# Where the second half of the queries and keys is set down on its way through a two-layer transformer kernel

## The chip, the cores and the metric

The kernel is one program on one core of a Trainium2 chip, written in Tile. A core has five engines that share an on-chip memory (SBUF, 128 partitions) and work through their own queues, each in its own order: TensorE (PE: matrix products, with weight loads listed apart as PEld), VectorE (DVE), ScalarE (ACT), GpSimd (POOL) and SyncE (SP), which here only issues transfers (DMA). TensorE's products go to a second memory (PSUM), from which VectorE and ScalarE take them here. The metric is the device time of one execution in microseconds (us).

## The reference, cut to what matters

A model width of 256, four sequences of 512 tokens, two layers, each an attention and a feed-forward part behind a layer norm, with residual sums:

```python
x = x + attn0(layernorm(x))   # 16 heads of 16, causal softmax over 512 tokens
x = x + ffn0(layernorm(x))    # 8 experts, weights from the two largest of a softmax per output column
x = x + attn1(layernorm(x))   # 16 heads of 128, 4 groups of keys and values
x = x + ffn1(layernorm(x))    # gated, 2048 wide, weights unpacked from 4 bits
```

The change lies in `attn0`, of which this is what counts:

```python
qkv = einsum('bsd,od->bso', x, w_project).reshape(b, s, 3, 16, 16)
q, k, v = transpose(qkv, (2, 0, 3, 1, 4))
att = softmax(where(causal, -1e9, einsum('bhqd,bhkd->bhqk', q, k) / 4), axis=-1)
out = einsum('bhqk,bhkd->bhqd', att, v)          # then a projection by w_out
```

## The kernel before, in words

The tokens are cut into four blocks (`NBLK`, j = 0 to 3) of 128 tokens from each of the four sequences. The attention of layer 0 runs in 44 batches, numbered n: block 0 has one batch for each sequence, block 1 two, blocks 2 and 3 four, since a later block has more keys and a batch then takes fewer groups of heads. A batch goes through `greatest` (scores, L647), `mask` (L660, with the row maxima on VectorE, L666), `shift` (a transposition `mxT`, L676, and the subtraction from the queries, L679), `powers` (the scores anew, L695, exponentials on ScalarE, L704, the mask on GpSimd, L714) and `mixed` (products with the values, `av`, L731). At the end of a sequence `divided` normalises (`av_T`, L749; `oq_T`, L766; a copy into `aT`, L769), and after the last sequence projects (`o`, L778, added to `xres` on VectorE, L788).

The rest of layer 0's work is filled in between. Python generators ("streams") yield pieces with a planned cost; `fill` takes pieces from them at fixed points of the loop over batches. The order of every engine's instructions is thus written out while the program is built (`manual_schedule`), and each engine keeps to it. A late instruction holds all that stands behind it on its engine. Streams that matter here:

- `prepare(j)` for blocks 2 and 3: layer norm, transposition (L582), then `projections(j)`.
- `fold_pieces`: adds the biases into the router's and the experts' weights (TensorE L252, VectorE L258). It reads the tile `rows`.
- `weight_pieces`: the experts' weights from the router's logits. Its first step writes `hi4` (VectorE, L371).
- `result_pieces`: the experts' products (`eo`, L234), scaled by ScalarE into `part` (L323), which VectorE adds up (L350 to L352).

`projections(j)` makes the block's queries and keys in two halves of the heads, `half` 0 and 1. Each half has two calls of `project`, i = 0 (keys) and 1 (queries). A call makes a product of 128 by 512 (`qk_ps`, two steps, L545), and ScalarE copies it from PSUM into the tile `stage` (L549). After the second call eight transfers (L555) carry the half from `stage` into its places in `qk`, where four heads lie at partitions 0, 32, 64 and 96. They are issued by SyncE (for block 0 half of them by ScalarE) and are 64 KB each.

`stage` has the size of 4 KB a partition and comes from the pool `a1`, which has one buffer for a tag. A tile of the same tag can be written only when all readers of the one before are done: here, when its eight transfers have landed. Block 0's first half alone is elsewhere (`unused`, in the space of the logits).

The pool `b1` holds the space of the experts, also one buffer for each tag. Two of its tags have 4 KB a partition as well: `hi4`, first used for the biases (`bs`), and then by `weight_pieces` from token group 0 on; and `part`, first used for `rows`, and then by `result_pieces`.

The products `qk_ps`, `oq_T`, `av_T`, the folds, the logits (`lg_ps`), the experts' products and `o` share two buffers of PSUM (`ps_dn`), so that a product can start when the last but one has been emptied. The scores have five buffers, of which four are filled at a time, and `mxT` and `av` share one.

Of the kernel before, what the change touches and what calls it, by code (L numbers as in the profile page):

```python
# [8 lines left out]
F32 = mybir.dt.float32  # L9
# [7 lines left out]
P = 128  # L17
# [15 lines left out]
def tile_transformer(  # L33
# [71 lines left out]
    b1 = w_ffn0.enter_context(tc.tile_pool(name="f0_1", bufs=1, side="right"))  # L105
# [8 lines left out]
    def need(engine, cost, gap=0, cond=None):  # L114
        return engine, cost, gap, cond
# [333 lines left out]
    with ExitStack() as l0:  # L449
# [90 lines left out]
        def project(j, xT, half, stage, i):  # L540

            at = 256 * (1 - i) + 128 * half
            ps = ps_dn.tile([P, 512], F32, tag="dn", name=f"qk_ps{j}_{half}_{i}")
            for hc in range(2):
                nc.tensor.matmul(  # L545
                    ps, lhsT=wp[:, hc, at : at + P],
                    rhs=xT[:, hc].rearrange("p s q -> p (s q)"), start=hc == 0, stop=hc == 1,
                )
            nc.scalar.copy(stage[:, i], ps)  # L549
            if i:  # L550
                to = 4 + j % 2
                for r in range(8):
                    h = 32 * (r % 4)
                    eng = nc.scalar if j == 0 and r % 2 else nc.sync
                    eng.dma_start(  # L555
                        out=qk[h + 4 : h + 20, 2 * half + r // 4, j : to + 1 : to - j].rearrange(
                            "p i s q -> p i (s q)"
                        ),
                        in_=stage[16 * r : 16 * r + 16],
                    )  # L560

        def values(j, xT, s):

            ps = ps_dn.tile([P, 2, HID], F32, tag="dn", name=f"v_ps{j}_{s}")
            for i in range(2):
                for hc in range(2):
                    nc.tensor.matmul(
                        ps[:, i], lhsT=xT[:, hc, s + i], rhs=wp[:, hc, 512:768],
                        start=hc == 0, stop=hc == 1,
                    )  # L570
            at = j * per_block
            to = va[:, at : at + per_block].rearrange("p (s h d) -> p s h d", s=NS, d=17)
            nc.scalar.copy(
                to[:, s : s + 2, :, 0:16], ps.rearrange("p s (h d) -> p s h d", d=16)
            )
# [14 lines left out]
        def projections(j, xT):  # L590
            if j > 1:
                for s in (0, 2):
                    yield need("PE", 1.75, 1, cond=lambda: blanked > 5 * j - 10)
                    values(j, xT, s)
            for half in range(2):
                if j or half:
                    stage = a1.tile([P, 2, 512], F32, tag="stage", name=f"stage{j}_{half}")
                else:
                    stage = unused("stage0", "p (i q) -> p i q", i=2)
                for i in range(2):  # L600

                    yield need(
                        "PE", 1.75, 0 if half or i else 1,
                        cond=lambda: j < 2 or done >= 8 * j - 12 and blanked >= 5 * j - 5,
                    )
                    project(j, xT, half, stage, i)
                if half == (not j) and j < 2:
                    for s in (0, 2):
                        yield need("PE", 1.75)
                        values(j, xT, s)  # L610

        def prepare(j):

            out = []
            yield from norm_pieces(
                j, b1, b2, out, cond=lambda: j == 2 or inputs[2].next is None
            )
            xT = a1.tile([P, 2, NS, P], F32, tag="xT0", name=f"xT0_{j}")
            yield from inputs_T(j, out[0], xT)
            yield from projections(j, xT)  # L620

        def unused(name, pattern, **sizes):

            tile = b2.tile([P, NE, HID], F32, tag="lg", name=name)
            return tile.rearrange("p e o -> p (e o)")[:, :1024].rearrange(pattern, **sizes)
# [188 lines left out]
        for piece in projections(0, xT):  # L814
            pass
# [3 lines left out]
        greatest(0)  # L819
        mask(0)  # L820
        inputs = {1: Stream(projections(1, xT))}
        done = blanked = 0
        fold = Stream(fold_pieces())
# [4 lines left out]
        for n in range(NBT):  # L828
            j, s, gs = batches[n]
# [92 lines left out]
    with ExitStack() as l1:  # L922
# [198 lines left out]
        for p in range(-1, NP):  # L1121
            j, kv = divmod(p, NKV)
# [179 lines left out]
```

## Time and profile before

| | us |
|---|---|
| median of 3 runs | 1177.23 |
| lowest, highest | 1175.32, 1181.05 |
| the profiled execution: its own time | 1182.05 |
| its span, first to last instruction | 1180.3 |
| TensorE busy in it | 1148.1 |
| VectorE busy | 809.7 |
| ScalarE busy | 484.3 |
| GpSimd busy | 108.1 |

The profiled execution's mean TensorE clock was 0.993 of full speed. The copies into `stage` (16 of them) start between 15.1 and 155.5 us of the span, and the transfers out of it between 17.4 and 161.0 us; a copy takes 586 ns, a transfer 2.4 us from its issue to its landing (median). So the change concerns the first seventh of the span; layer 0's attention and all that follows come after it.

How to read the rows of the profile that follow: a row of the timeline has the start in us, the duration in us (of all merged instructions), the engine, the line of the kernel, the operation, the tiles (output, then inputs), shapes and the number of instructions, and in brackets how long the engine sat idle before it and what ended this. A row of the waits has the engine and line that waited, what it waited for, and the total in us, the number of times and the longest. A row of the table by stretches has the stretch, its length, and for PE, PEld, DVE, ACT and POOL the busy time with the number of instructions; then the granted TensorE clock, the share of the DMA engines and the rate in GB/s.

### The profile page before, as it was taken

The page shows a single profiled execution, that of the slowest core. Times are in us where ns is not written, and L with a number is a line of the kernel's source. Part 1 is how long each engine was busy: PE and PEld are TensorE (multiplying, and loading weights), DVE is VectorE, ACT ScalarE, POOL GpSimd, SP SyncE. Part 2 cuts the span into 40 slices and gives each one's busy share as a digit, 9 for nine tenths or more (in the row PEclk, how much of TensorE's full clock was granted, in tenths as well). Part 3 has the DMA queues.
Part 4 walks back from the last instruction along what each step waited for, and adds up shares of the span by engine and source line. Part 5 has one row for each costly group of instructions (what it writes and reads, how often), then busy time and mean ns, then how long its engine had stood idle before and what let it go on. Part 6 is the DMA issues. An engine that isn't in the chain of part 4 may idle for free.

```text
span 1180.3 us, 18580 instructions
## 1 busy us (share of the span) xinstructions
PE 1148.1 (97%) x7178; PEld 663.9 (56%) x7178; DVE 809.7 (69%) x1783; ACT 484.3 (41%) x1099; POOL 108.1 (9%) x152
## 2 busy tenths in 40 slices
PE   7999989999999899999999999999999999999998
PEld 3656545555555445555555556565644465485487
DVE  5656869999989872867872685687599844725710
ACT  1434545555565453444444443555244312303300
POOL 7313212111111100000000000000000000000000
PEclk9989989999999999999999999999999999999999
DMA  7320010000000320000000001020020000000000
GB/s 217 68 67 12 10 28 1 1 1 2 2 1 2 113 66 1 1 1 1 1 1 1 1 1 45 19 58 24 21 50 3 0 1 18 0 1 18 1 13 23
DMA packets 21239, 26.46 MB, mean 22 GB/s; under 512 B 5128, under 2 KB 14600, under 8 KB 21152
## 3 DMA queue, kind: packets, MB, share of 16 engines
q1 hardware_dynamic: 20480, 24.10, 7.6%
q10 hardware_dynamic: 672, 1.18, 0.4%
q8 instruction: 56, 0.92, 0.3%
q14 instruction: 31, 0.25, 0.1%
HBM read 18.97 MB, written 2.10 MB: 18 GB/s over the span
## 4 chain that ended last, share of the span: by engine, by line
PE 79%; DVE 15%; ACT 2%; issue 2%; POOL 1%; DMA 1%; SPq 0%; ACTq 0%; DVEq 0%; POOLq 0%
PE qk_ps L982 11%; PE y L1229 9%; PE o L1073 9%; PE g L911 9%; PE u L911 9%; PE lg_ps L234 8%; PE eo L234 7%; DVE mx L666 3%; PE s L647 3%; PE s L695 3%; PE av L731 2%; PE qk_ps L545 2%; PE v_ps L964 2%; PE a L1053 1%; PE s L995 1%
## 5 line engine op out<-in xcount | busy, mean ns | idle before, releaser
L982 PE MATMUL qk_ps<-xT,wqkv 128*128 128x512 f32 x320 | 148.9, 599 | 2.3 <-ACT part L323 1.2
L234 PE MATMUL lg_ps<-rw,xT 128*128 128x512 f32 x256 | 122.5, 601 | 1.3 <-ACT xT L949 0.3
L234 PE MATMUL eo<-ew,xT 128*128 128x512 f32 x256 | 121.5, 600 | 0.8 <-ACT lg L297 0.5
L1073 PE MATMUL o<-wpj,oT 128*128 128x256 f32 x512 | 119.1, 382 | 0.0
L1229 PE MATMUL y<-wd,it 128*128 128x256 f32 x512 | 111.8, 379 | 0.0
L1073 PEld LDWEIGHTS o<-wpj,oT 128*128 128x128 f32 x512 | 95.9, 190 | 27.5 <-issue 14.3
L1229 PEld LDWEIGHTS y<-wd,it 128*128 128x128 f32 x512 | 97.0, 190 | 15.0 <-issue 2.2
L666 DVE TENSOR_REDUCE mx<-s 128x1 f32<-128x384 f32 (+3 forms) x176 | 100.4, 631 | 1.4 <-PE s L660 1.4
L982 PEld LDWEIGHTS qk_ps<-xT,wqkv 128*128 128x128 f32 x320 | 59.1, 190 | 71.4 <-issue 57.4
L704 ACT ACTIVATE pt<-s 128x512 f32<-128x512 f32 (+1 forms) x176 | 84.1, 564 | 36.3 <-PE s L695 36.3
L911 PE MATMUL g<-xT,wgu 128*128 128x512 f32 x192 | 90.4, 593 | 0.0
L911 PE MATMUL u<-xT,wgu 128*128 128x512 f32 x192 | 90.2, 592 | 0.0
L323 ACT ACTIVATE part<-eo,c 128x256 f32<-128x256 f32 x128 | 53.6, 472 | 84.7 <-PE eo L234 77.1
L714 POOL TENSOR_SCALAR_AFFINE_SELECT pt<-pt 128x256 f32<-128x256 f32 (+2 forms) x88 | 62.8, 720 | 261.9 <-ACT pt L704 261.3
L1207 ACT ACTIVATE th<-sq 128x512 f32<-128x512 f32 x64 | 40.3, 630 | 87.6 <-DVE sq L1206 87.6
L234 PEld LDWEIGHTS lg_ps<-rw,xT 128*128 128x128 f32 x256 | 46.1, 190 | 46.1 <-issue 37.3
L234 PEld LDWEIGHTS eo<-ew,xT 128*128 128x128 f32 x256 | 46.1, 190 | 45.7 <-issue 38.3
L222 DVE TENSOR_TENSOR xres<-xres,y 128x256 f32<-128x256 f32 x16 | 6.7, 421 | 92.5 <-PE y L1229 92.5
L185 POOL TENSOR_TENSOR ln_rs<-rs_v,minus_half 128x4 f32<-128x4 f32 x16 | 17.6, 1100 | 552.2 <-DVE rs_v L184 439.8
L297 ACT COPY lg<-lg_ps 128x512 f32<-128x512 f32 x64 | 37.6, 588 | 73.5 <-PE lg_ps L234 73.5
L1208 DVE SCALAR_TENSOR_TENSOR th<-th,g 128x512 f32<-128x512 f32 x63 | 43.1, 684 | 29.3 <-ACT th L1207 29.2
L911 PEld LDWEIGHTS u<-xT,wgu 128*128 128x128 f32 x192 | 36.5, 190 | 45.9 <-issue 44.7
(233 smaller groups left out, 1784.4 us busy)
## 6 DMA issues: line engine op xcount, KB each, us to landing
qk<-stage SPq DMA_DIRECT2D x56, 64.0 KB, 2.4
wqkv<-in_w_qkv SPq DMA_DIRECT2D x8, 320.0 KB, 6.6
rw<-in_router_w SPq DMA_DIRECT2D x8, 256.0 KB, 6.9
ew<-in_expert_w SPq DMA_DIRECT2D x8, 256.0 KB, 5.0
wpj<-in_w_proj SPq DMA_DIRECT2D x1, 2048.0 KB
out<-xres SPq DMA_DIRECT2D x4, 512.0 KB, 2.6
xres<-in_x SPq DMA_DIRECT2D x3, 512.0 KB, 8.5
dq_wgu<-in_gate_w SPq DMA_DIRECT2D x8, 128.0 KB, 2.4
```

Source lines behind the costliest of these rows:

```text
L234: nc.tensor.matmul(ps, lhsT=xT[:, hc, (g % 4) * P : (g % 4 + 1) * P], rhs=w[:, hc, 2 * pair : 2 * pair + 2, :].rearrange("p e o -> p (e o) ...
L297: nc.scalar.copy(lg[:, 2 * pair : 2 * pair + 2, :].rearrange("p e o -> p (e o)"), ps)
L323: nc.scalar.mul(part[:, e % 4], ps[:, i], c[:, e : e + 1])
L666: nc.vector.tensor_reduce(maxes[n % 2][:, h, gs[0] : gs[0] + nb], ps[:, : nb * nk].rearrange("p (b k) -> p b k", b=nb), AX.X, ALU.max,)
L704: nc.scalar.activation(pt[:, i, : nb * nk], tiles[2 * pair + i][:, : nb * nk], AF.Exp, scale=0.25)
L714: nc.gpsimd.affine_select(out=last, in_=last, compare_op=ALU.is_ge, fill=0.0, base=0, pattern=pattern, channel_multiplier=-1,)
L911: nc.tensor.matmul(ps, lhsT=wgu[:, w, half, jj, par * P : (par + 1) * P], rhs=xT[:, half, :], start=half == 0, stop=half == 1,)
L982: nc.tensor.matmul(ps, lhsT=wqkv[:, hc, kv, h, :], rhs=xT[:, hc, :], start=hc == 0, stop=hc == 1,)
L1073: nc.tensor.matmul(ys[t // 2][:, t % 2], lhsT=state["o"][:, h, t * P : (t + 1) * P], rhs=wpj[:, HPK * kv + h, :], start=kv == 0 and h == 0 ...
L1207: nc.scalar.activation(th, sq, AF.Tanh, scale=0.7978845608028654)
L1208: nc.vector.scalar_tensor_tensor(th, th, 1.0, gp, ALU.add, ALU.mult)
L1229: nc.tensor.matmul(ps, lhsT=it[:, c // 2, c % 2, t * P : (t + 1) * P], rhs=wd[:, c // 2, c % 2, :], start=c == 0, stop=c == 2 * NJ - 1,)
```

## The change

The second halves of blocks 2 and 3 no longer take the one `stage` buffer of `a1`. The second half of block 2 is set down in the buffer of the tag `hi4`, and that of block 3 in the buffer of the tag `part`, both in `b1`. First halves and the second half of block 1 stay in `stage`. The size and the layout within the tile, the copies and the transfers are as before.

```diff
             for half in range(2):
-                if j or half:
+                if j > 1 and half:
+
+                    stage = b1.tile(
+                        [P, 2, 512], F32, tag="hi4" if j == 2 else "part", name=f"stage{j}_1"
+                    )
+                elif j or half:
                     stage = a1.tile([P, 2, 512], F32, tag="stage", name=f"stage{j}_{half}")
                 else:
                     stage = unused("stage0", "p (i q) -> p i q", i=2)
```

With it the users of a buffer stand in another row. `hi4`: the biases, then the half of block 2, then the first `hi4` of `weight_pieces`. `part`: `rows`, then the half of block 3, then the first `part` of `result_pieces`. `stage`: the second half of block 1, then the first half of block 2, then the first half of block 3. The order of instructions on the engines and on SyncE is the same as before; what differs is what some of them wait for.

## The prediction

> **What bounds the kernel now.** I read the page first, for the engine that is busy and for its clock; then the waits of the stretch in which the change lies; then the instructions in order of time around the two longest of those waits; last a table of short stretches, for the clock.
>
> The page (busy share by engine; mean granted TensorE clock in 40 slices of 29.5 us):
>
> ```profile
> PE 1148.1 (97%) x7178; PEld 663.9 (56%) x7178; DVE 809.7 (69%) x1783; ACT 484.3 (41%) x1099; POOL 108.1 (9%) x152
> ...
> PEclk9989989999999999999999999999999999999999
> ```
>
> TensorE is the bound nearly everywhere, so time is to be had only where it stands still or runs slowly. Its clock is below nine tenths in two slices only, the third (59 to 89 us) and the sixth (148 to 177 us). The waits between 55 and 175 us (engine and line waited for: total us, times, longest):
>
> ```profile
> DVE qk L679 <- PE mxT L676: 18.4, 4, 10.9
> ...
> ACT stage L549 <- DMA qk<-stage: 9.3, 2, 4.7
> ...
> DVE ew L258 <- PE fold L252: 6.1, 2, 4.9
> PE qk_ps L545 <- ACT stage L549: 6.0, 2, 3.2
> ```
>
> Two waits of the copy into `stage` for transfers out of `stage` make two waits of TensorE for that copy, and VectorE waits behind TensorE. The first in order of time (start us, duration), with the undisturbed first half of block 2 ahead of it for comparison:
>
> ```profile
> 68.42 0.38 PE L766 MATMUL oq_T<-ident,oq 128*128 128x128 f32 x2
> 68.64 1.88 PE L545 MATMUL qk_ps<-xT,wp 128*128 128x512 f32 x4
> ...
> 71.68 1.17 PE L695 MATMUL s<-qk 32*128 32x128 f32 x32
> ...
> 76.98 0.38 PE L766 MATMUL oq_T<-ident,oq 128*128 128x128 f32 x2
> ...
> 79.57 0.59 ACT L549 COPY stage<-qk_ps 128x512 f32<-128x512 f32 x1 [4.58 <-DMA qk<-stage]
> ...
> 80.21 3.78 PE L545 MATMUL qk_ps<-xT,wp 128*128 128x512 f32 x4 [2.85 <-ACT stage L549]
> ...
> 86.21 1.18 PE L695 MATMUL s<-qk 32*128 32x128 f32 x32
> ```
>
> The same four matmuls take 1.88 us at 68.64 and 3.78 us at 80.21. The wait costs twice: TensorE stands, and then runs at half speed. The second place is block 3:
>
> ```profile
> 148.14 0.39 PE L766 MATMUL oq_T<-ident,oq 128*128 128x128 f32 x2
> ...
> 151.09 0.59 ACT L549 COPY stage<-qk_ps 128x512 f32<-128x512 f32 x1 [4.71 <-DMA qk<-stage]
> ...
> 151.73 3.78 PE L545 MATMUL qk_ps<-xT,wp 128*128 128x512 f32 x4 [3.20 <-ACT stage L549]
> ...
> 158.25 1.99 PE L778 MATMUL o<-wo,aT 128*128 128x256 f32 x8
> ```
>
> The clock by stretches (the figure after POOL's) gives how long half speed lasts:
>
> ```profile
> 78.00:80.00 2.00, 0.00 (x0) 0.00 (x0) 1.56 (x3) 0.43 (x1) 0.00 (x0) 0.86 0.21 37
> 80.00:82.00 2.00, 1.79 (x2) 0.84 (x3) 0.00 (x0) 0.43 (x2) 0.00 (x0) 0.50 0.00 0
> ...
> 86.00:88.00 2.00, 2.00 (x43) 1.62 (x36) 0.00 (x0) 0.90 (x3) 0.00 (x0) 0.93 0.53 89
> ...
> 150.00:152.00 2.00, 0.27 (x1) 0.27 (x2) 2.00 (x9) 0.91 (x4) 0.00 (x0) 0.78 0.08 13
> ...
> 156.00:158.00 2.00, 2.00 (x40) 1.58 (x36) 0.00 (x0) 0.40 (x2) 0.00 (x0) 0.51 0.20 30
> ```
>
> A mean of 0.86 over 2 us at the levels 1.0 and 0.5 is 0.56 us of half speed, so it begins at 79.44; 0.93 gives its end, 86.28. Likewise 151.12 to 157.96. Each lasts 6.84 us.
>
> **The change: what it removes.** In blocks 2 and 3 the second half's copy no longer waits for the first half's eight transfers. Nothing is added or moved: each engine and SyncE keep their instructions and their order, so no queue is passed and no transfer added. The copies (586 ns) only write elsewhere.
>
> First place. Undisturbed, `oq_T` to the score matmuls of L695 takes 71.68 - 68.42 = 3.26 us; here it takes 86.21 - 76.98 = 9.23. Gain 5.97 us: 3.01 is standing (80.21 - 76.98, less the usual 68.64 - 68.42 = 0.22), 2.96 is half speed (86.21 - 80.21 = 6.00, against 71.68 - 68.64 = 3.04). What is late next, if the copy isn't? Its matmuls ran from 73.28 to 75.16 and ScalarE's exponentials end at 74.99, so it runs at 75.2 and ends at 75.8; `oq_T` at 76.98 and the fold of VectorE that ends at 76.69 are no later than before. Then projection at 77.2, `av` at 79.2, L695 at 80.2; the maxima that free its score banks end at 79.56, 0.7 us earlier. VectorE stood 4.89 us for a fold and 3.62 us for L778, so it follows.
>
> Second place. From the projection the neighbour at 140.83 takes 1.87 us to `av`; `av` of 24 matmuls takes 0.79 (165.01 to 165.80), L695 0.88 (143.71 to 144.59): 3.54 us. With 0.22 from `oq_T` that is 3.76 against 158.25 - 148.14 = 10.11. Gain 6.35 us: 3.37 standing, 2.98 half speed. Late next: the projection's matmuls end at 146.96, so the copy runs from 147.0 to 147.6; six sums of L415 follow it on ScalarE (2.41 us, their last input made at 148.5) to 150.0, then the copy of `aT` to 150.4, which L778 needs at 151.9: 1.5 us to spare. Maxima end at 150.55, L695 starts at 151.0. VectorE has done its work at 152.3 and stood 10.86 us for `mxT` at 162.75; that comes at 156.4, and it still stands some 4 us.
>
> Together 6.4 us standing and 5.9 us half speed: 12.3. At both places the other engines wait behind TensorE too and no load from memory is due, so nothing later keeps its old time and the gain reaches the end. The saving is covered by no other work.
>
> **The waits it adds.** (a) The first `hi4` of the experts' weights (L371, VectorE, 128.54; all of VectorE queues behind it) waits for the transfers out of the stage of block 2. These are issued from about 80 to 86.5 and land 2.4 us later: over 30 us to spare. (b) The first product of the experts (L323, ScalarE, 171.82, so 165.5 on the same scale with the second gain) waits for the transfers of block 3's: copy done at 151.0, eight issues in 6.2 us as from 156.20 to 162.37, landing 2.4 later, 159.6: 5.9 us to spare. (c) In block 2 `oq_T` takes the PSUM bank of the copy at 75.2 to 75.8 (1.1 us early), and the projection after it that of the fold ending at 76.69 (0.5 us early). Missing these costs the excess alone, 0 to some 0.5 us. I take 0 for all.
>
> **Row against rule.** The half-speed term is where a rule speaks against me. The Trainium skill, "TensorE: Matmul & The Clock Gate", "Why this matters for your kernels", asks for no TensorE gap over about 3 us; its "What's actually happening" puts the drop after an idle window of about 3.4 us. The first gap is 77.36 to 80.21, 2.85 us: by the rule no clock is lost and the sum is 6.4. The rows show the clock lost at both places, so I use 12.3. The same section says the windows run free at 3413 ns. This trace agrees: half speed lasts 6.84 us, two windows, and its two starts lie 71.68 us apart, 21.0 windows. The window that ends at 79.44 held 2.08 us of standing and was enough. So whether a gap costs clock depends on how it falls into windows, and can differ from run to run.
>
> **The number.** Against the profiled execution's own time, 1182.05 us (span 1180.3 and 1.75 around it): 1169.7. It stands 4.8 above the median of the runs, 1177.23, and those span 1175.32 to 1181.05, 5.7 us, about what two losses of 3.0 would make. I read the standing (6.4) as in every run and the clock loss as by chance. If 2.08 us in one window is needed, a gap of 2.85 us meets that in 0.62 of the phases, one of 3.2 us in 0.72 (estimates from the gaps and the window); 1.3 losses of 3.0 are 4.0 in the median run. 1177.2 - 6.4 - 4.0 = 1166.8, which I call 1167.
>
> **Rivals.** (1) The median run carries no clock loss: gain 6.4, 1170.8. For: the rule, and that the median lies far below the profiled run. Against: both gaps lose clock in the one run that shows it. (2) One stall comes back in another form, at the tightest point: `aT` behind the six sums on ScalarE holds L778, or a PSUM bank holds the projection. One place yields little: gain 3 to 6, about 1172.5. Against: the margins above; a lateness costs its excess only. (3) Slower: the borrowed `part` tile. L323 waits for eight transfers, ScalarE's queue behind it stops, TensorE runs out of PSUM banks and loses its clock again (3 us). It begins to cost when the transfers land over 5.9 us later than 159.6, and eats the whole gain when they hold L323 by 9.3 us, that is 15 us late: 17.7 us to land, where the slowest of `stage` took 4.0. Held for 15.2 us it makes about 1183. (4) That the change doesn't act: excluded as far as the copy waits only for its matmul and for tiles long done (zeros of the biases, folds before 90 us).
>
> **How the numbers follow.** The forecast 0.77, by itself 1162.5 to 1169.5; rival 1 0.12; rival 2 0.08; rival 3 0.03. Range: below, both clock losses in the median run (1164.9) less 3 for the spread between runs; above, rival 1 and half of rival 2: 1162 to 1172.5. Half a per cent, about what a measurement of this kernel can tell from no change, is 5.9 us, 1171.3. Faster: 0.77, two thirds of rival 1 and a quarter of rival 2, 0.87; same 0.10; slower 0.03.
>
> **What would show it.** Right: no wait of `stage` for DMA after 55 us; a clock of 1.00 in every stretch from 60 to 170; the projection 0.2 us after `oq_T` at both places and 1.9 us long; L371 and L323 waiting for no DMA; a profiled span near 1168. Wrong: a clock below 1.00 there though TensorE has no gap; `aT` or a PSUM bank as the new releaser of TensorE; L323 released by `stage`; a gain at 90 us or 160 us that is no longer there at 400.

## The result, and the profile after

The changed kernel takes 1170.42 us (median of 4 runs, 1169.60 to 1170.83), the kernel before 1177.14 (4 runs, 1175.32 to 1181.05): a ratio of 0.994, 95% interval 0.9919 to 0.9962. Set against 31 runs of the kernel before on one chip, whose median is 1178.77, it is 0.9925 (0.9908 to 0.9941) at 1170.31. So it is faster by 7 to 9 us, 0.6 to 0.75 per cent. The forecast said 1167; the range of all its cases was 1162 to 1172.5.

In the page of the changed kernel, TensorE is busy 6.1 us less, and no slice of its clock is below nine tenths (mean granted clock 1.000, before 0.993; span 1168.6 us, before 1180.3):

```profile
PE 1142.0 (98%) x7178; PEld 661.5 (57%) x7178; DVE 809.8 (69%) x1783; ACT 484.3 (41%) x1099; POOL 108.4 (9%) x152
...
PEclk9999999999999999999999999999999999999999
```

The waits from 55 to 165 us (total us, times, longest). The lines are five later than before, so L684 is the former L679, and L700, L771 and L783 are L695, L766 and L778:

```profile
DVE qk L684 <- PE mxT L681: 12.0, 4, 4.9
...
ACT stage L549 <- PE qk_ps L545: 5.3, 6, 1.6
...
ACT part L323 <- PE eo L234: 3.8, 2, 3.4
...
DVE ew L258 <- PE fold L252: 1.2, 1, 1.2
```

In this stretch `stage` now waits for its products alone, never for a transfer. TensorE's wait for the copy is gone, VectorE's longest wait for `mxT` fell from 10.9 to 4.9, and that for the fold from 4.9 to 1.2. L323, the next user of `part`, waits for its product and not for the borrowed space, and L371, the next user of `hi4`, does not wait for a transfer when it first writes there, at 123.2 us. The two places in the timeline (start, duration):

```profile
77.59 0.38 PE L771 MATMUL oq_T<-ident,oq 128*128 128x128 f32 x2
...
77.81 1.88 PE L545 MATMUL qk_ps<-xT,wp 128*128 128x512 f32 x4
...
80.85 1.17 PE L700 MATMUL s<-qk 32*128 32x128 f32 x32
```

```profile
142.77 0.39 PE L771 MATMUL oq_T<-ident,oq 128*128 128x128 f32 x2
...
143.00 1.88 PE L545 MATMUL qk_ps<-xT,wp 128*128 128x512 f32 x4
...
146.49 1.99 PE L783 MATMUL o<-wo,aT 128*128 128x256 f32 x8
```

From `oq_T` to L700 3.26 us, where it took 9.23; from `oq_T` to L783 3.72, where it took 10.11. Together 12.36 us. The span is only 11.7 shorter, because this execution reached the first place 0.61 us later than the one before (77.59 against 76.98), ahead of anything the change touches. From L783 on both take the same: 1168.6 - 146.49 = 1022.1 and 1180.3 - 158.25 = 1022.1. Nothing is given back in the remaining seven eighths.

So the two profiled executions agree with the sum. What doesn't agree is the time without a profile: 7 to 9 us, not 12. The experiments ask where the difference lies.

### The profile page after: what moved, and what is told of

The parts are those of the page before. It is cut to its first block, busy times and chain, and to the rows that moved or that the text cites. A ratio compares the mean times of both kernels' runs of the same rounds, so it can differ in the third digit from the quotient of the medians.

```text
span 1168.6 us, 18563 instructions
## 1 busy us (share of the span) xinstructions
PE 1142.0 (98%) x7178; PEld 661.5 (57%) x7178; DVE 809.8 (69%) x1783; ACT 484.3 (41%) x1099; POOL 108.4 (9%) x152
## 4 chain that ended last, share of the span: by engine, by line
PE 81%; DVE 13%; ACT 2%; issue 1%; POOL 1%; DMA 0%; SPq 0%; ACTq 0%; DVEq 0%; POOLq 0%
PE qk_ps L987 11%; PE y L1234 9%; PE o L1078 9%; PE g L916 9%; PE u L916 9%; PE lg_ps L234 8%; PE eo L234 7%; PE s L652 3%; PE s L700 3%; DVE mx L671 3%; PE av L736 2%; PE v_ps L969 2%; PE qk_ps L545 2%; PE a L1058 1%; PE s L1000 1%
## 5 line engine op out<-in xcount | busy, mean ns | idle before, releaser
L323 ACT ACTIVATE part<-eo,c 128x256 f32<-128x256 f32 x128 | 53.7, 472 | 85.2 <-PE eo L234 75.2
```

The costliest lines, as they stand in the source:

```text
L323: nc.scalar.mul(part[:, e % 4], ps[:, i], c[:, e : e + 1])
```

## The experiments

"Standing" is the time in which TensorE does nothing because the copy is late; a "loss" is what half speed costs after it. Theory A: the standing is in every run of the kernel before; the half speed is in some runs, more or less of it, by how the gaps fall into the clock's windows. Theory B: both are in every run. Theory C: part of the gain is given back further on.

**The changed kernel again, for the clock of every run** (no edit).

> The changed kernel once more, for the clock of every run of it and of the kernel before. Theory A (standing is saved in every run, the clock loss only where a run of before had it): every run of the changed kernel at clock 1.000 and within 1.5 us of 1170.4; runs of before spread over some 6 us, and their times follow their clocks: about 1176.5 at 1.000, about 1179 with one loss (0.997 to 0.998), about 1182 with two (0.993 to 0.995); median difference 6 to 9 us. Theory B (both losses occur in every run of before, and the profiled execution was long for another reason): before at 0.993 to 0.995 in every run, times without relation to the clock. Theory C (the standing is given back further on): a run of before at clock 1.000 lies within 3 us of the changed kernel.

Measured: all 6 runs of the changed kernel at a granted clock of 1.000, 1169.18 to 1170.64. The kernel before, by the clock of each run; these are the 31 runs of this experiment and 50 made beside later ones:

| mean clock of the run | runs | median us | lowest, highest |
|---|---|---|---|
| 1.000 | 6 | 1175.68 | 1175.24, 1176.34 |
| 0.999 | 7 | 1178.33 | 1176.99, 1178.76 |
| 0.996 to 0.998 | 56 | 1178.25 | 1176.33, 1181.06 |
| 0.994 to 0.995 | 7 | 1180.31 | 1179.74, 1180.93 |
| 0.993 | 5 | 1181.85 | 1181.72, 1182.16 |

The time follows the clock (correlation -0.82). The mean clock is a coarse measure: 3.41 us at half speed take 0.0015 from it (3.41 x 0.5 / 1177), and half speed after TensorE's last product counts as well, so that 0.999 can be one loss (the first of the two further executions below) or none (the run with 11 products). Only 5 of 81 runs are like the profiled one, and 6 show no loss. That is A, and B is out. A run without loss still stands 5.4 us above the changed kernel (1175.68 - 1170.31), more than the 3 that C allowed, so C is out. Over all 81 the mean is 1178.59: 2.9 us of clock loss in the average run.

**Each half of the change alone.**

```diff
-                if j > 1 and half:
+                if j == 2 and half:      # the other run: j == 3
```

> Only block 2's second half set down in hi4; block 3's stays in stage. Theory A: 3.0 us of standing saved in every run and the chance of one clock loss gone: 3 to 4.5 us under the median of before, runs at clock 1.000 or 0.997 to 0.998 and never 0.993. Theory C: less than 1.5 us. In the profile: no wait of stage for DMA near 79 us, the one near 146 as before, about 4.7 us on ScalarE and 3.2 us on TensorE.

> Only block 3's second half set down in part. Theory A: 3.4 us of standing saved in every run, 3.4 to 5 us under the median of before; with the run of block 2 alone it adds up to the whole change, 6 to 9 us. If block 3's borrowed tile costs something (L323 held), this one gains less than block 2's alone.

Measured: block 2 alone 1175.64 (ratio 0.9969, 0.9957 to 0.9981), clocks 0.996 to 1.000; block 3 alone 1174.84 (0.9961, 0.9950 to 0.9973), clocks 0.997 to 1.000. Medians 3.1 and 3.9 us under that of before, each within its expectation. The product of the ratios is 0.9930, with the whole change at 0.9925: within the intervals the halves add up (the medians alone add up to 7.1 of 8.5 us), and no cost of a borrowed tile shows. The clock of 0.996 is lower than one loss was expected to make it; the last run below shows what else lowers it. Each profile keeps exactly one wait for a transfer after 55 us. In that of block 2 alone it is the second:

```profile
143.01 0.39 PE L771 MATMUL oq_T<-ident,oq 128*128 128x128 f32 x2
146.38 3.45 PE L545 MATMUL qk_ps<-xT,wp 128*128 128x512 f32 x4 [2.97 <-ACT stage L549]
```

**The wait left in, the standing filled.** Here TensorE gets products without use behind `oq_T`, at the two places of the kernel before. They go into a half, added to the PSUM tile of `oq_T`, that nothing reads:

```diff
-            ps = ps_dn.tile([P, 2, P], F32, tag="dn", name=f"oq_T{j}_{s}")
+            ps = ps_dn.tile([P, 4, P], F32, tag="dn", name=f"oq_T{j}_{s}")
             ...
+            if j < 2 and s == NS - 1:
+                for i in range(FILL):
+                    nc.tensor.matmul(
+                        ps[:, 2:4].rearrange("p k q -> p (k q)"), lhsT=ident, rhs=wp[:, 0, :256],
+                        start=not i, stop=i == FILL - 1,
+                    )
+            ps = ps[:, 0:2]
```

First with FILL = 11:

> The kernel before with both waits left in, and 11 products of 128 by 256 (0.24 us each, 2.6 us together) behind oq_T at the two places, into an unused half of its PSUM tile, so that TensorE works where it stood. Nothing else is changed. Theory A: the waits stay as long, but no run loses clock: all runs at 1.000 and within 1.5 us of each other, at 1176 to 1177, the fast end of before; the median 0 to 3 us under that of before, the changed kernel still 6 us faster. Theory B: 6 us under before, since the clock loss is in every run of it. If the clock is not lost by the standing but by something else there, the profile keeps 0.5 after each wait.

Measured: 1179.60, 14 runs at clock 0.999 to 1.000 and within 1.6 us of each other, but 3 us slower than expected. A miss of size: each of the products is two matmuls in the trace and takes 0.45 us, where 0.24 was expected, so that the eleven outlast the wait:

```profile
77.69 4.91 PE L772 MATMUL oq_T<-wp,ident 128*128 128x256 f32 x22
82.44 1.88 PE L546 MATMUL qk_ps<-xT,wp 128*128 128x512 f32 x4
```

That is 4.97 us from `oq_T` (77.47) to the projection, 4.75 over the usual 0.22, at each place: 9.5 above the changed kernel's 1170.3 gives 1179.8. It already says what the clock hangs on: `stage` still waited for the transfers, TensorE worked meanwhile, and the profile shows no half speed and the runs little spread. With FILL = 6:

> As the run with 11 products, of which each turned out to take 0.45 us, not 0.24, so that they outlasted the wait by some 2 us at each place; here 6 of them, 2.7 us, just under the wait. Both waits stay. Theory A (clock lost by the standing, in part of the runs): every run at clock 1.000 or 0.999, spread under 1.6 us, median 1176 to 1177.5: 6 to 7 over the changed kernel (the bare standing) and 1.5 to 3 under the median of before (the clock losses). Theory B (standing and half speed are worth 12 together in every run): 1170 plus 6, but before 6 above it in every run. If the clock is lost for another reason than standing: as before, clocks down to 0.993.

Measured: 1175.81 (20 runs, 1175.17 to 1177.19; ratio to before 0.9981, 0.9974 to 0.9987), 18 of them at clock 1.000 and two at 0.999; before beside it 1178.18. The median is 0.2 us under the expected 1176 to 1177.5, and the spread is 2.0 us, not the expected 1.6. The first place in its trace:

```profile
77.32 0.38 PE L767 MATMUL oq_T<-ident,oq 128*128 128x128 f32 x2
77.54 2.75 PE L772 MATMUL oq_T<-wp,ident 128*128 128x256 f32 x12
80.42 1.98 PE L546 MATMUL qk_ps<-xT,wp 128*128 128x512 f32 x4
...
83.56 1.17 PE L696 MATMUL s<-qk 32*128 32x128 f32 x32
```

The projection starts no earlier than in the kernel before, but runs at full speed. `oq_T` to L696 takes 6.24 us: 2.98 over the changed kernel, and 2.99 under the 9.23 of before. The other place takes 152.41 - 145.48 = 6.93, 3.21 over. This separates the two costs: the standing alone is 5.5 us in the time (1175.81 - 1170.31), 6.2 in the traces; the clock loss is 2.4 between the medians. (The two profiled executions themselves lie 5.87 us apart, 1176.17 against 1170.30, and this one reached the first place 0.27 us earlier.) TensorE doing useless work in the gap makes the kernel faster by 0.2%.

With FILL = 3, so that part of the gap stays:

> 3 products, 1.35 us, behind oq_T at both places: TensorE still stands, but 1.5 to 1.8 us instead of 2.9 to 3.2. Theory A with the window rule as the prediction used it (about 2.1 us of standing in one window costs the clock): no loss, clock 1.000 to 0.999 in all runs, time as with 6 products within 0.5 us. If half that standing is enough, some runs lie at 0.996 to 0.998 and 1.7 to 3 us higher.

Measured: 1176.26 (22 runs), clocks 0.999 to 1.000, 0.45 us from FILL = 6. Gaps of 1.22 and 1.65 us in its profile cost no clock:

```profile
81.06 1.98 PE L546 MATMUL qk_ps<-xT,wp 128*128 128x512 f32 x4 [1.22 <-ACT stage L550]
...
149.46 1.99 PE L546 MATMUL qk_ps<-xT,wp 128*128 128x512 f32 x4 [1.65 <-ACT stage L550]
```

**Two further profiled executions of the kernel before** (no edit).

> The kernel before, one more profiled execution, for another position of its two standing times in the clock's windows. Theory A: each stretch at half speed begins where a window of 3.41 us with at least 2.1 us of standing ends, starts lie a whole number of windows apart, and a stretch lasts one or two windows. Time between 1175.5 and 1182.2, by the number and length of the stretches.

> The kernel before, a further profiled execution; expectations as for b1.

Measured: 1178.55 and 1179.57. In the first one the first place loses clock and the second does not:

```profile
78.00 0.38 PE L766 MATMUL oq_T<-ident,oq 128*128 128x128 f32 x2
81.10 3.59 PE L545 MATMUL qk_ps<-xT,wp 128*128 128x512 f32 x4 [2.72 <-ACT stage L549]
...
151.22 1.98 PE L545 MATMUL qk_ps<-xT,wp 128*128 128x512 f32 x4 [2.96 <-ACT stage L549]
```

The longer gap, 2.96 us against 2.72, is the harmless one. The stretches of this execution (the clock is the third figure from the right) say where the windows lie:

```profile
80.00:82.00 2.00, 0.90 (x2) 0.39 (x3) 0.57 (x1) 0.86 (x2) 0.00 (x0) 0.83 0.00 0
...
84.00:86.00 2.00, 2.00 (x38) 0.88 (x36) 0.97 (x2) 0.59 (x1) 0.00 (x0) 0.82 0.00 0
```

0.83 and 0.82 give half speed from 81.32 to 84.72: 3.40 us, one window where the prediction's profile had two. The window before it, from 77.91, held the whole first gap. Twenty windows of 3.413 us after 81.32 a boundary falls at 149.58, inside the second gap (148.26 to 151.22), and cuts it into 1.32 and 1.64 us: no loss. In the other execution both places lose one window:

```profile
80.00:82.00 2.00, 1.20 (x2) 0.68 (x3) 0.14 (x1) 0.86 (x2) 0.00 (x0) 0.59 0.00 0
82.00:84.00 2.00, 2.00 (x4) 0.65 (x3) 0.00 (x0) 0.00 (x0) 0.00 (x0) 0.56 0.00 0
...
152.00:154.00 2.00, 2.00 (x22) 0.88 (x24) 0.00 (x0) 1.75 (x8) 0.00 (x0) 0.51 0.01 4
154.00:156.00 2.00, 2.00 (x37) 1.50 (x30) 0.00 (x0) 0.30 (x2) 0.00 (x0) 0.64 0.32 50
```

Half speed from 80.36 to 83.76 and from 152.04 to 155.44; the starts lie 71.68 us apart, 21.0 windows, as in the first profile of before. The second of these windows held 2.04 us of standing, a little less than the 2.1 that was expected to be needed. `oq_T` to L695 or L778 here takes 7.83 and 8.48 us, of which 3.01 and 3.12 are standing: these losses cost about 1.6 us each, and the one above 1.8, where the long ones of the prediction cost 3.0.

**The borrowed tile with the nearest next user.**

```diff
-                        [P, 2, 512], F32, tag="hi4" if j == 2 else "part", name=f"stage{j}_1"
+                        [P, 2, 512], F32, tag="hi4", name=f"stage{j}_1"
```

> The changed kernel with block 3's second half set down in hi4 as well, not in part. The next user is then not L323 at about 160 us but the first step of the experts' weights of token group 1 (L371, VectorE), 154.3 us in the profile of the changed kernel, with all of VectorE behind it; the eight transfers land at about 153.9 (issues end at 151.5, 2.4 later). If a borrowed tile costs only what its next user is held by, this one is at the edge: 0 to 1 us over the changed kernel, clock 1.000 in every run. If the borrowed tile has a cost of its own, or VectorE's hold is multiplied behind it, 2 us or more. Rival 3 of the prediction at its nearest point.

Measured: 1170.11 (5 runs, 1169.98 to 1170.77; ratio to before 0.9930, 0.9916 to 0.9943), the same as the changed kernel, clocks 0.999 to 1.000. VectorE at that point (start, duration):

```profile
153.66 0.17 DVE L437 SCALAR_TENSOR_TENSOR c<-sums,c 128x8 f32<-128x8 f32 x1
154.03 1.23 DVE L371 TENSOR_TENSOR hi<-lg 128x1024 f32<-128x1024 f32 x1 [0.21 <-issue]
```

The last of the eight transfers lands at 153.15 us in this trace, and VectorE is done with L437 at 153.8: no wait for a transfer, only 0.21 us of passing the semaphores. Later TensorE waits 0.24 us for VectorE (`av` at 159.71), too little to show between the medians. So even the nearest next user comes after the transfers have landed, and the slower rival has no ground here. A user that comes before the landing was not tried.

One part of the expectation failed: the clock was to be 1.000 in every run, and two of the five have 0.999, the profiled one among them. It is at half speed from 192.00 to 195.41, one window, though TensorE did not stand:

```profile
189.88 2.14 PE L652 MATMUL s<-qk 32*128 32x384 f32 x7
...
192.63 3.32 PE L234 MATMUL lg_ps<-rw,xT 128*128 128x512 f32 x4
```

```profile
190.00:192.00 2.00, 2.00 (x9) 0.93 (x8) 2.00 (x5) 1.83 (x6) 1.20 (x2) 1.00 0.00 0
192.00:194.00 2.00, 2.00 (x8) 1.35 (x8) 1.93 (x3) 0.00 (x0) 1.16 (x1) 0.50 0.00 0
```

The window before it, from 188.59, holds almost nothing but scores, products over 32 of the 128 partitions. The run of block 2 alone has the same loss at the same products, from 197.14 to 200.56. The other nine profiles run these products at full clock; that it hangs on how the windows cut them is likely but not shown. The loss costs nothing in the end: this execution is 0.24 us ahead of the changed kernel's at these scores, 0.37 behind at 198, and 0.29 ahead at the next `oq_T` (201.16 against 201.45), where TensorE of the changed kernel waits 0.55 us for VectorE.

## Why the prediction was right or wrong

- **What bounds, and where.** Right. Both waits, and nothing else, are what the change took away.
- **The change removes two waits and adds none that is felt.** Right: both projections start 0.22 or 0.23 us after `oq_T` and take 1.88, the clock is 1.00 at both places, L371 and L323 are held by no transfer. Copies of ScalarE came when the steps said: the first one was forecast 1.8 us ahead of `oq_T`, and starts 1.78 ahead of it (75.81 against 77.59). `aT` was forecast 1.5 us ahead of L778 and its copy ends at 144.9, 1.6 ahead.
- **The sum of the trace, 12.3 us.** Right to 0.1: 12.36 measured at the two places, and none of it is lost later in the profile.
- **The step to the median of the runs.** Wrong in size. The prediction took 6.4 of standing and 1.3 losses of 3.0, that is 4.0, off 1177.2. Standing is 5.5 us in the runs (6.2 in the traces; where the other 0.7 lies is open, but profiled executions reach the first place anywhere from 76.98 to 78.16 us, so the start varies by more than that). The loss is mis-sized too: 3.0 was read from the one profile at hand, where both losses lasted two windows. A loss of one window costs 1.6 to 1.8. The average run of before loses 2.9, not 4.0, which is 1.1 of the miss. Another 1.4 is luck of the draw: the four runs of before with their median of 1177.14 lie only some 1.5 above those without loss, where the median of 81 is 1178.34. 0.9, 1.1 and 1.4 together are the 3.4 us by which 1167.0 fell short. The time lies above the span that the forecast had for itself, 1162.5 to 1169.5, and inside the whole range.
- **The better step stood in the prediction.** The profiled execution less its own two losses and its own standing is 1182.05 - 12.3 = 1169.7, and with the late start of 0.61 us it is 1170.3, what the changed kernel takes. The changed kernel has no gap at the two places, and all of its ten runs have a clock of 1.000; the chance belonged to the time before, and had not to be carried over to the time after. (The late start could not be foreseen.)
- **Row against rule.** The row was right to be taken: losses come from gaps of 2.7 to 3.2 us. The Trainium skill, "TensorE: Matmul & The Clock Gate", "Why this matters for your kernels", sets about 3 us; in the runs here 1.96 us of standing in one window was enough. (Even by that rule the second gap of 3.20 us was no clear case, so the prediction's "by the rule 6.4" holds for the idle window of 3.4 us only.) Of the same page's "What's actually happening" the free-running window of 3413 ns is borne out in all profiles of the kernel before (starts 21.0 windows apart in two of them, a harmless second gap where the count puts a boundary in the third).
- **Rivals.** The time fell on the first one's number (1170.8), but not by its mechanism: the profiles and clocks show the losses, they are only shorter on average and rare at full length. The second and third did not happen, the third not even at its nearest point. The sum of the third took 12.3 as the whole gain, although the forecast took only 10.4 off the median.

## What to carry to other kernels

A wait that stops TensorE can cost twice, by the standing and by half speed after it. Here the first was in every run, and the second hung on where the gap fell among the clock's windows, so one profile shows one draw of it: list the granted clock of every run before sizing it, and look in a profile where the clock falls, since a loss at a place where TensorE waits for others anyway costs nothing. If a change takes the gap away altogether, subtract from the profiled execution what that execution lost, not an average loss from a median. And a single buffer that is emptied by transfers can borrow space whose next user comes later than the transfers land; the run with both halves in `hi4` shows that half a microsecond of margin is enough.

## What the runs showed of the hardware

- At the two places the clock drops at the end of a window of 3.41 us in which TensorE stood 1.96 us (block 3 alone: from 77.52 to 79.48), 2.04, 2.08 or more, seven cases in all. It does not drop with 1.64 us in a window, nor with gaps of 1.22 and 1.65. At the end of the program 1.84 us did not drop it either (the run with FILL = 6: the last product ends at 1170.36, a window ends at 1172.20, and the clock falls one window later, at 1175.62). So half a window, 1.71 us, is not the limit for standing.
- Standing is not the only thing that drops it: in two of eleven profiles it fell after a window without standing that held almost only products over 32 partitions. Why is open.
- The clock can drop after TensorE has resumed work: in the execution with 3.59 us of projection it worked from 81.10 and lost speed at 81.32.
- Half speed lasted one window where at most 0.44 us of it was standing (six cases, the two without standing before them among these), and two where it was 0.61, 0.77 and 0.84 us.
- Products without use, issued into the gap, keep the clock up: 2.4 us between medians for six of them at each of two places.
